# A Performer whose state is kept in a rotated basis, with weights turned on the chip

## The chip, the cores and the metric

One core of a Trainium2 chip runs the whole program; nothing is shared with other cores. The metric is device time in microseconds (us) of one execution. Everything is float32. On this core TensorE (PE) multiplies matrices, VectorE (DVE) and ScalarE (ACT) work elementwise and read its results out of PSUM, GpSimd (POOL) works on SBUF, and SyncE's queue (SP) issues nearly all DMAs.

## The reference

The input x is 8 images of 128 channels and 16 x 16 positions. Four layers follow each other; each is added to what it got, except that layer 1 adds its input inside.

```python
x = x + adder2d(group_norm(x), W)               # layer 0: -sum |W - patch|, 3x3, 128 to 128 channels
x = layer1(x)                                   # layer 1: three selective scans (f, b, s), their attention, two 3x3 convolutions
t = tokens(x)                                   # 8 x 256 tokens of 128 features
t = t + attention(ln(t)); t = t + moe(ln(t))    # layer 2
t = t + performer(ln(t))                        # layer 3, first half
t = t + spectral(ln(t))                         # layer 3, second half
```

The Performer is what most of this change touches:

```python
h = x @ tok_W + tok_b + pe
for i in range(8):
    u = layer_norm(h, ln1_g[i], ln1_b[i])       # eps 1e-5, mean and variance over the 128 features
    q, k, v = u @ Wq[i] + bq[i], u @ Wk[i] + bk[i], u @ Wv[i] + bv[i]
    ...                                         # rotary, random features (44 of each of 8 heads), linear attention
    h = h + o @ Wo[i] + bo[i]
    u = layer_norm(h, ln2_g[i], ln2_b[i])
    h = h + gelu(u @ W1[i] + b1[i]) @ W2[i] + b2[i]
    if i == 3:
        h = gelu(h @ enc_W + enc_b) @ dec_W + dec_b
return tanh(h)
```

In layer 1, for each image: `q, k, v` are the results of the three scans; `out_a = v @ softmax(q.T @ k).T` goes through a 3x3 convolution (`fuse1`, 256 to 128 channels), the gated sum of the three goes through `out_proj`, and a second 3x3 convolution (`fuse2`) takes both, 256 to 128 channels.

## The kernel before

The program runs the layers one after the other. Features lie on the 128 partitions, the 2048 tokens on the free axis, in four blocks of 512 tokens (two images each). A 128x512 result fills one bank of PSUM. A float32 product is recorded as two matmul records.

**Layer 1** (`_scans`, lines 492 to 840) walks over 192 states: 4 pairs of images, 3 branches, 16 states each. Per state DVE does two scans (L815) and a multiplication by C (L826; in the states `AWAY` POOL does it), and PE adds two products to `acc` (L834). All engines but SP follow the order of the program here (`manual_schedule`). What else has to be done is written as generators and drawn in between: `more` prepares the unit (pair and branch) after the next, and `other` runs `beside()`: norms, gates, the attention of a finished pair (`F.images`) and its two convolutions of 18 products each (`F.convolutions`). Each state has a `room` of `SHARE` = 2 products for both together, and a generator also stops for the state at every `LATER`. What is left of `other` after the last state is run in a loop behind it (L838). In `beside()` the convolutions of pairs 0 and 1 stand behind their images; those of pair 2 don't. They are drawn in `mamba_layer` (L448 to L458), after the scans, two steps for each round over the last pair's two attention generators. Behind them come the last pair's gates (`F.gated`) and convolutions. This tail is ordered by a scheduler, not by the program's order.

**The Performer** (`performer_layer`, L1002) has one generator per block, `_block`, with layer 2 in its first 30 steps. `AHEAD` takes these 30 steps of blocks 0 and 1 at the priority of layer 1's tail. Then `ORDER`, a string of 1132 digits, says which block makes its next step, and the four computing engines take their instructions in just this order. Each block has two PSUM banks of its own, and the layers' weights (`lw`) have two buffers for all blocks.

A norm (`_norm`, L1141) takes three steps: a product with `center` (identity minus 1/128) into PSUM and its squares by ACT; a product of the squares with `mean` (1/128 everywhere), Ln and Exp by ACT; and DVE's product of both, for the layers' norms followed by DVE's affine with gain and bias (L1166). For the attention's norm DVE also sums u over the tokens of an image (L1162), and `L1409` applies the affine to these sums. The block that reaches a layer first loads its weights (`_layer`, `_Layer`, L1299), 948 KB, and adds bv @ Wo to the output bias. ACT holds one function table at a time; a change between the table with Ln and Exp and the table with Gelu and Tanh is a table load (L1079).

In an attention, the step called pn below is the last product before the division: 32 records into two banks and ACT's Ln and Exp of the denominator; the steps before it transpose the query features (`turned`, L1499, records named px).

The functions that the change touches, and what calls them:

Of the kernel before, what the change touches and what calls it, by code (L numbers as in the profile page):

```python
# [45 lines left out]
RATIO = M ** -0.5  # L46
# [12 lines left out]
for _k, _n in (("q", P), ("k", P), ("v", NPAIR * (PD + 2)), ("o", P), ("w1", DFF), ("w2", DFF), ("f", HM)):  # L59
    _a = LW[next(reversed(LW))].stop if LW else 0  # L60
    LW[_k] = slice(_a, _a + _n)
# [14 lines left out]

def _constants():

    p = np.arange(P)
    c = {}  # L80
    c["ident"] = np.eye(P, dtype=np.float32)
    c["group"] = (p[:, None] // 4 == p[None, :] // 4).astype(np.float32) / 1024.0

    sel = np.zeros((P, 2, 4, NH), np.float32)
    for n in range(2):
        sel[:, n, n, :] = 0.25 * (p[:, None] // DH == np.arange(NH)[None, :])
    c["sel"] = sel.reshape(P, 8 * NH)
    c["mask"] = (np.minimum(p // M, 1)[:, None] == np.arange(PD)[None, :] // DH).astype(np.float32)
    c["pe"] = _fixed_pos_emb(P, L).T
    lpe = _fixed_pos_emb(DH, L)  # L90

    c["sin"] = np.tile(np.repeat(lpe[:, : DH // 2], 2, axis=-1).T, (NH, 1)) * np.where(p % 2, -1.0, 1.0).astype(np.float32)[:, None]
    c["cos"] = np.tile(np.repeat(lpe[:, DH // 2 :], 2, axis=-1).T, (NH, 1))
    c["more"] = np.isin(p % FG, MORE).astype(np.float32)[:, None]
    c["rev8"] = np.tile(np.arange(NE, 0, -1, dtype=np.float32), (P, 1))
    c["rev4"] = np.tile(np.arange(4, 0, -1, dtype=np.float32), (P, 1))
    return c
# [12 lines left out]
def _vectors(x):  # L110
# [19 lines left out]
    col("tok_b", x["L3_attn_tok_b"])  # L130
    col("enc_b", x["L3_attn_enc_lin_b"])
    col("dec_b", x["L3_attn_dec_lin_b"])
    for i in range(NL):
        for n in ("ln1_g", "ln1_b", "bq", "bk", "bv", "bo", "ln2_g", "ln2_b", "b1", "b2"):
            col(f"{n}{i}", x["L3_attn_" + n][i])
    return v
# [18 lines left out]
def _weights(x):  # L155
# [20 lines left out]
    for h in range(NH):  # L176
# [5 lines left out]
        [wq, wk, wv.reshape(NL, P, -1), x["L3_attn_Wo"], x["L3_attn_W1"]]  # L182
# [254 lines left out]
def mamba_layer(E):  # L437
# [3 lines left out]
    with ExitStack() as ctx:  # L441
# [7 lines left out]

        convs = F.convolutions(last - 1)  # L450
        images = [F.attention(last, b) for b in range(UB)]
        while images:
            images = [g for g in images if next(g, 0) != 0]
            for _ in range(2):
                next(convs, None)
        for p in (convs, F.gated(last), F.convolutions(last)):
            for _ in p:
                pass  # L458
# [33 lines left out]
def _scans(E, ctx, F):  # L492
# [266 lines left out]
    def beside():  # L759
# [13 lines left out]
        for p in range(NPAIRS - 1):  # L773
            yield from until((p + 1) * pair)
            if p == 1:
                yield from norm(3)
            yield from F.images(p)
            if p < NPAIRS - 2:
                yield from F.convolutions(p)
                yield from gates(p + 2)  # L780
# [221 lines left out]
def performer_layer(E, W):  # L1002
# [4 lines left out]
    with ExitStack() as ctx:  # L1007
# [18 lines left out]
        S.lw = enter("plw", 2)  # L1026
        own(2)
# [4 lines left out]
        S.lb = one.tile([P, NL], F32, tag="lb", name="lb")  # L1032
        for i in range(NL):
            nc.gpsimd.tensor_scalar_mul(S.lb[:, i : i + 1], S.v(f"ln1_b{i}"), float(L))
        S.layers = {"2": _Layer2(S)}

# [19 lines left out]
    "3213231232131213023213021023021023121301131131231231023110311131312132113211331331313331030102030213"  # L1056
    "0031203023203022020200220032030230323301332013203320323302301332303131032132302232213101231123120322"
    "3002201300220312023101311322302231312012103310233021313123020013210232112032313200331002122323212013"
    "2032302203120132202310130121023201120032013212300120011230211302132110323310133230133201233023331321"
    "0320032103232020231302023120313230131021020122102210210112101120230203201120030103112312113210132303"  # L1060
    "3131323013102012013013031233102100331003320120232021031021032013321302210220232022032120112023112031"
    "0232031200132103100133121131013121031120303130313001023213123320103203203202033220322103130103123032"
    "1302213222132211321120210212130112030230231230102011321100321103101201233010330213100231021003212203"
    "0221202032103122332322322332102210320213130112021102120130201310201133231121012001023002123112030132"
    "0212020201002102013022033222031032233203310221020302213102331223331020310330123131011203013002031230"
    "1031231112031231102312023212032123210300221030222300232312032323101203231331333032033203302121330230"
    "32330022303003321023122313133021"
# [73 lines left out]
def _norm(S, src, g=None, b=None, sums=None):  # L1141

# [4 lines left out]
    sq = S.many.tile([P, BLK], F32, tag="t", name="lsq3")  # L1147
    act(S, sq, xc, AF.Square)
# [8 lines left out]
    if sums is None:  # L1157
        nc.vector.tensor_mul(u, xc, sq)  # L1158
    else:
        for q in range(2):  # L1160
            cols = slice(q * L, (q + 1) * L)
            nc.vector.scalar_tensor_tensor(  # L1162
                u[:, cols], xc[:, cols], 1.0, sq[:, cols], ALU.mult, ALU.mult, accum_out=sums[:, q : q + 1]
            )
    if g is not None:
        nc.vector.tensor_scalar(u, u, g, b, ALU.mult, ALU.add)  # L1166
# [131 lines left out]

class _Layer:  # L1299


    def __init__(self, S, i):
        nc = S.nc
        self.w = S.lw.tile([P, LW_COLS], F32, tag="w", name=f"lw{i}")
        nc.sync.dma_start(self.w, S.dram["layers"][i])

        pb = bank(S, [P, 1], "pb3")
        S.mm(pb, self["o"], S.v(f"bv{i}"))
        self.bo = S.lw.tile([P, 1], F32, tag="bo", name="bo3")
        nc.vector.tensor_add(self.bo, pb, S.v(f"bo{i}"))  # L1310
# [5 lines left out]
def _layer(S, i):  # L1316
    if i not in S.layers:
        S.layers[i] = _Layer(S, i)
    return S.layers[i]


def _block(S):
# [10 lines left out]
        S.v("tok_b"),  # L1333
# [3 lines left out]
    )  # L1337
    yield
    for i in range(NL):
        yield from _attention(S, i, h)  # L1340
        w = _layer(S, i)
        u = yield from _norm(S, h, S.v(f"ln2_g{i}"), S.v(f"ln2_b{i}"))
# [11 lines left out]
        nc.vector.scalar_tensor_tensor(h, p2, S.v(f"b2{i}"), h, ALU.add, ALU.add)  # L1354
        yield
        if i == NL // 2 - 1:
            pz = bank(S, [LAT, BLK], "pz3")
            S.mm(pz, S.w["enc"], h)
# [5 lines left out]
            nc.vector.tensor_scalar_add(h, ph, S.v("dec_b"))  # L1364
            yield
    th = one.tile([P, BLK], F32, tag="u", name="th")
    act(S, th, h, AF.Tanh)
# [7 lines left out]
def _attention(S, i, H):  # L1375
# [8 lines left out]
    sums = one.tile([P, 2], F32, tag="us", name="us3")  # L1384
    u = yield from _norm(S, H, S.v(f"ln1_g{i}"), S.v(f"ln1_b{i}"), sums)
    w = _layer(S, i)
# [21 lines left out]

    nc.vector.tensor_scalar(sums, sums, S.v(f"ln1_g{i}"), S.lb[:, i : i + 1], ALU.mult, ALU.add)  # L1409
# [155 lines left out]
    nc.vector.scalar_tensor_tensor(H, po, w.bo, H, ALU.add, ALU.add)  # L1565
    yield

# [182 lines left out]
```

## Time and profile before

| What | Value |
|---|---|
| median of 3 runs | 3107.86 us (3105.3 to 3108.57) |
| profiled execution | 3111.2 us |
| its span | 3109.4 us |
| mean granted clock of TensorE | 0.987 |
| scans of layer 1 | 989 to 1740 us of the span |
| tail of layer 1 | 1740 to 1815 |
| layer 2 of blocks 0 and 1 alone | 1815 to 1896 |
| Performer (and the end of layer 2) | 1896 to 2866 |
| spectral layer | 2866 to 3109 |

Times inside the execution count from the start of the span. A row of a group reads: line, engine, operation, what is written and read, shapes, count | busy time in us, mean duration in ns | idle time of that engine just before, and what ended it. A matmul's duration in such a row is its latency; in a full queue the next one starts earlier, so that prices of products are taken from runs of many records. A row of a stretch reads: the stretch and its length, then the busy time and the count of PE, PE's weight loads (PEld), DVE, ACT and POOL, the granted clock, the share of the DMA engines and GB/s.

### The profile page before, as it was taken

To read this page: it belongs to the slowest core of one execution; us is meant where nothing else is said; L and a number is where in the kernel's file an instruction comes from. 1 tells how busy PE (TensorE), PEld (TensorE's weight loads), DVE (VectorE), ACT (ScalarE), POOL (GpSimd) and SP (SyncE) were. 2 spreads that over 40 slices of the span, in tenths; PEclk is the share of its full clock that TensorE was granted. 3 is DMA by queue.
4 is the path that set the end of the run, shared out by engine and by line. 5 is a ranking of instruction groups with operands and counts; after the bars stand their busy time and mean duration, and the time that the engine had idled before them with its cause. 6 is when DMAs were issued, how large, how long until landed. Compare 5 with 4: busy or idle time off the path is not lost.

```text
span 3109.4 us, 42495 instructions
## 1 busy us (share of the span) xinstructions
PE 2918.6 (94%) x16686; PEld 1294.9 (42%) x16686; DVE 2483.7 (80%) x3507; ACT 2204.1 (71%) x2634; POOL 706.1 (23%) x393
## 2 busy tenths in 40 slices
PE   6999999999999788998997889999999999999999
PEld 2333332333332233443443444455555555554444
DVE  6999999999996899999999437886877787785431
ACT  5999999999996787778777234467677777767111
POOL 3000000000000799999998200000000000000110
PEclk9999999999999899999999999999999999999999
DMA  1000000000000444344444100000000000001100
GB/s 39 1 1 5 1 1 5 1 1 5 1 1 4 167 150 144 140 152 136 138 149 136 51 28 1 13 1 14 14 13 1 14 13 1 13 1 38 54 27 14
DMA packets 39198, 131.47 MB, mean 42 GB/s; under 512 B 7491, under 2 KB 10573, under 8 KB 37589
## 3 DMA queue, kind: packets, MB, share of 16 engines
q1 hardware_dynamic: 38564, 128.02, 12.2%
q8 instruction: 131, 2.15, 0.3%
q10 hardware_dynamic: 432, 0.73, 0.1%
q14 instruction: 71, 0.57, 0.1%
HBM read 125.85 MB, written 1.84 MB: 41 GB/s over the span
## 4 chain that ended last, share of the span: by engine, by line
PE 68%; DVE 16%; ACT 7%; POOL 4%; issue 3%; DMA 1%; DVEq 0%; ACTq 0%; POOLq 0%
PE o L265 30%; PE p L265 7%; DVE st L815 5%; PE acc L265 4%; PE g L265 4%; PE conv L265 3%; PE var L265 2%; PE pf L265 2%; POOL dbu L729 2%; PE xc L265 2%; PE pc L265 2%; PE pq L265 2%; PE pn L265 1%; PE pconv L265 1%; PE px L1502 1%
## 5 line engine op out<-in xcount | busy, mean ns | idle before, releaser
L265 PE MATMUL o<-d,sel 128*32 128x512 f32 x8800 | 946.5, 592 | 5.5 <-DVE d L405 5.5
L407 ACT ACTIVATE d<-sh,w 128x2048 f32<-128x2048 f32 x460 | 886.3, 1996 | 64.3 <-PE o L265 54.4
L405 DVE TENSOR_SCALAR d<-sh,w 128x2048 f32<-128x2048 f32 x640 | 789.4, 1292 | 48.9 <-PE o L265 39.7
L729 POOL TENSOR_TENSOR dbu<-du,bs 128x1024 f32<-128x1024 f32 x191 | 447.0, 2367 | 997.3 <-DMA cs<-rows 991.4
L265 PEld LDWEIGHTS o<-d,sel 128*32 128x32 f32 x8800 | 298.2, 110 | 653.0 <-issue 541.5
L815 DVE TENSOR_TENSOR_SCAN st<-da,dbu 128x512 f32<-128x512 f32 x384 | 446.2, 1206 | 18.3 <-POOL dbu L729 15.0
L265 PE MATMUL acc<-st,cst 128*128 128x512 f32 x768 | 377.4, 623 | 62.8 <-DVE st L826 62.6
L742 ACT ACTIVATE da<-delta,neg_a 128x510 f32<-128x510 f32 x384 | 256.8, 684 | 79.0 <-DVE st L815 77.7
L265 PEld LDWEIGHTS acc<-st,cst 128*128 128x128 f32 x768 | 144.5, 196 | 264.8 <-issue 141.7
L1611 POOL COPY u<-u 128x512 f32<-128x512 f32 x4 | 2.5, 613 | 1035.3 <-DVE u L1158 1035.3
L826 DVE TENSOR_TENSOR st<-st,pcs 128x1024 f32<-128x1024 f32 x168 | 205.2, 1222 | 18.2 <-ACT pcs L734 0.8
L1079 ACT ACT_TABLE_LOAD x132 | 169.4, 1283 | 2.3
L1682 ACT COPY ug<-p 128x512 f32<-128x512 f32 x64 | 37.5, 586 | 178.2 <-PE p L265 178.2
L734 ACT COPY pcs<-cs 128x512 f32<-128x512 f32 x168 | 97.8, 582 | 54.3 <-DVE st L826 48.7
L265 PE MATMUL conv<-pad,f 128*128 128x512 f32 x288 | 132.6, 596 | 1.9 <-ACT pad L991 1.3
L265 PE MATMUL p<-g,lw 128*128 128x512 f32 x256 | 119.6, 612 | 8.8 <-ACT g L1087 8.8
L265 PE MATMUL p<-u,lw 128*128 128x512 f32 x256 | 122.6, 602 | 3.7 <-ACT g L1087 2.8
L399 DVE SCALAR_TENSOR_TENSOR d<-sh,w,d 128x2048 f32<-128x2048 f32 x52 | 122.3, 2352 | 1.9
L265 PE MATMUL p<-T,H 128*128 128x512 f32 x256 | 113.7, 596 | 4.1 <-DVE ug L1684 3.8
L265 PE MATMUL g<-ug,me 128*128 128x512 f32 (+1 forms) x320 | 112.1, 509 | 0.2 <-DVE ug L1684 0.2
L1087 ACT ACTIVATE ex<-ex 128x352 f32<-128x352 f32 x128 | 62.8, 494 | 68.5 <-DVE ex L1495 67.2
L1492 DVE TENSOR_REDUCE mq<-pq 128x8 f32<-128x352 f32 x128 | 66.4, 519 | 41.4 <-PE pq L265 41.0
(316 smaller groups left out, 4031.6 us busy)
## 6 DMA issues: line engine op xcount, KB each, us to landing
bs<-rows SPq DMA_DIRECT2D x96, 512.0 KB, 3.8
cs<-rows SPq DMA_DIRECT2D x96, 512.0 KB, 4.7
m<-in_Mphi SPq DMA_DIRECT2D x8, 1024.0 KB, 4.8
lw<-in_layers SPq DMA_DIRECT2D x8, 948.0 KB, 4.6
f<-in_fuse SPq DMA_DIRECT2D x2, 1152.0 KB, 7.5
T<-in_T SPq DMA_DIRECT2D x1, 2064.0 KB, 7.9
x<-in_x SPq DMA_DIRECT2D x4, 256.0 KB, 6.0
total<-sums SPq DMA_DIRECT2D x16, 64.0 KB, 2.0
```

The costliest lines, as they stand in the source:

```text
L265: self.nc.tensor.matmul(out, lhsT=lhsT, rhs=rhs, start=start, stop=stop)
L399: nc.vector.scalar_tensor_tensor(held, tap(k), w[:, k, f : f + 1], held, ALU.max, ALU.add)
L405: nc.vector.tensor_scalar(d, tap(k), wk, None, ALU.max)
L407: nc.scalar.activation(d, tap(k), AF.Abs, scale=-1.0, bias=wk)
L729: gen.tensor_tensor(dbs[r], got[r // NST]["du"], bc(row("bs", r), 1, 2), ALU.mult)
L734: nc.scalar.copy(pcs[r], row("cs", r))
L742: nc.scalar.activation(das[g % 3][:, :, 1:], d[:, :, 1:], AF.Exp, scale=a)
L815: nc.vector.tensor_tensor_scan(st[:, h, :], da, dbs[r][:, h, :], 0.0, ALU.mult, ALU.add)
L826: nc.vector.tensor_tensor(st, st, bc(pcs[r][:, :], 1, 2), ALU.mult)
L1079: S.tc.keep_in_program_order(S.nc.scalar.preload_act_table_set(name))
L1087: S.nc.scalar.activation(out, src, func, **kw)
L1492: nc.vector.tensor_reduce(mq, f, AX.X, ALU.max)
```

## The change

Three things are changed together.

**The basis.** The Performer's state h is kept as R.T h, where R is a Householder reflection whose last column is the constant 1/sqrt(128). The last row of the rotated state is then sqrt(128) times the mean over the features, and the other 127 rows hold the centred part. A norm therefore needs no product with `center`: the squares of the state are taken straight from SBUF, the variance is a product over 127 rows, and u is the 127 rows times the reciprocal deviation. Row 127 of u holds the constant 1, set once, and row 127 of `sums` the constant 256.

**The weights.** What reads u is turned on the chip: for Wq, Wk, Wv and for W1 a matrix `m` = R with its rows scaled by the gain, and its last column replaced by the bias, is multiplied with the weights on PE and copied back over them by ACT. Gain and bias of the norms so disappear into the weights. What writes the state (Wo, W2, tok, dec) is turned by `_outputs_turned`: a sum over the outputs and a rank-one correction on DVE and POOL. Biases and enc are turned once, in `_rotated_state`. At the end one product with R per block turns the state back for tanh. The turning of a layer's weights is three more steps in block 0's generator for each of the eight layers, and only block 0 loads them.

**The order.** `ORDER` is a new string, of 1092 digits. And the convolutions of pair 2 stand in `beside()` behind the pair's images, as those of pairs 0 and 1 do; the tail of `mamba_layer` only draws the two images, the gates and the last convolutions.

The diff, cut to its core:

```diff
@@ mamba_layer
-        convs = F.convolutions(last - 1)
         images = [F.attention(last, b) for b in range(UB)]
         while images:
             images = [g for g in images if next(g, 0) != 0]
-            for _ in range(2):
-                next(convs, None)
-        for p in (convs, F.gated(last), F.convolutions(last)):
+        for p in (F.gated(last), F.convolutions(last)):
...
@@ beside
             yield from F.images(p)
+            yield from F.convolutions(p)
             if p < NPAIRS - 2:
-                yield from F.convolutions(p)
                 yield from gates(p + 2)
...
@@ performer_layer
         S.lw = enter("plw", 2)
+        S.turn = enter("pturn", 1)
...
-        S.lb = one.tile([P, NL], F32, tag="lb", name="lb")
-        for i in range(NL):
-            nc.gpsimd.tensor_scalar_mul(S.lb[:, i : i + 1], S.v(f"ln1_b{i}"), float(L))
         S.layers = {"2": _Layer2(S)}
+        _rotated_state(S, blocks[0])
...
+def _outputs_turned(S, w, rows=P):
+    nc = S.nc
+    n = w.shape[1]
+    a, b = (S.turn.tile([P, n], F32, tag=f"t{j}{n}", name=f"turn{j}")[0:rows] for j in range(2))
+    nc.vector.tensor_reduce(a, w, AX.X, ALU.add)
+    nc.vector.tensor_scalar_mul(a, a, ROOT)
+    nc.vector.tensor_tensor(b, a, w[:, :, MEAN], ALU.subtract)
+    nc.vector.tensor_scalar_mul(b, b, ROOT / (1.0 - ROOT))
+    nc.gpsimd.tensor_tensor(w, w, bc(b, 2, P), ALU.subtract)
+    nc.gpsimd.tensor_copy(w[:, :, MEAN], a)
...
 class _Layer:
     def __init__(self, S, i):
+        self.w = S.lw.tile([P, LW_COLS], F32, tag="w", name=f"lw{i}")
+        S.nc.sync.dma_start(self.w, S.dram["layers"][i])
+
+    def turned(self, S, i):
...
+        _outputs_turned(S, self.w[:, LW["o"].start : LW["w2"].stop].rearrange("p (n d) -> p n d", d=P))
+        for n, cols in (("ln1", slice(0, LW["v"].stop)), ("ln2", LW["w1"])):
+            m = S.turn.tile([P, P], F32, tag=n, name=n + "m")
+            nc.gpsimd.tensor_scalar_mul(m, S.c("rot"), S.v(f"{n}_g{i}"))
+            nc.gpsimd.tensor_copy(m[:, MEAN:P], S.v(f"{n}_b{i}"))
+            pw = bank(S, [P, cols.stop - cols.start], "pw3")
+            S.mm(pw, m, self.w[:, cols])
+            nc.scalar.copy(self.w[:, cols], pw)
+            yield
         pb = bank(S, [P, 1], "pb3")
         S.mm(pb, self["o"], S.v(f"bv{i}"))
...
+def _state_norm(S, h, sq, u, sums=None):
+    nc = S.nc
+    rest = slice(0, MEAN)
+    var = bank(S, [P, BLK], "var3")
+    S.mm(var, S.mean[rest, :], sq[rest, :])
+    act(S, sq, var, AF.Ln, bias=S.eps)
+    act(S, sq, sq, AF.Exp, scale=-0.5)
+    yield
+    if sums is None:
+        nc.vector.tensor_mul(u[rest], h[rest], sq[rest])
+    else:
...
@@ _block
+    sq = _squares(S, h)
+    yield
+    if S.t == 0:
+        yield from _weights_of(S, 0)
+    u = one.tile([P, BLK], F32, tag="u", name="un3")
+    sums = one.tile([P, 2], F32, tag="us", name="us3")
+    nc.gpsimd.memset(u, 1.0)
+    nc.gpsimd.memset(sums, float(L))
     for i in range(NL):
-        yield from _attention(S, i, h)
-        w = _layer(S, i)
-        u = yield from _norm(S, h, S.v(f"ln2_g{i}"), S.v(f"ln2_b{i}"))
+        sq = yield from _attention(S, i, h, sq, u, sums)
+        w = S.layers[i]
+        yield from _state_norm(S, h, sq, u)
...
+        if i + 1 < NL:
+            sq = _squares(S, h)
             yield
+            if S.t == 0:
+                yield from _weights_of(S, i + 1)
+    yield
+    ph = bank(S, [P, BLK], "ph4")
+    S.mm(ph, S.c("rot"), h)
     th = one.tile([P, BLK], F32, tag="u", name="th")
-    act(S, th, h, AF.Tanh)
+    act(S, th, ph, AF.Tanh)
...
@@ _attention
-    nc.vector.tensor_scalar(sums, sums, S.v(f"ln1_g{i}"), S.lb[:, i : i + 1], ALU.mult, ALU.add)
```

The matrix R joins the constants as `rot` (128 columns), the position code is rotated on the host, in the layers' weights W1 stands before Wo so that what is turned alike lies together, and the output biases move into one group of columns, `added`.

## The prediction

> **What bounds the kernel now.** I read the page first, then the busy time by stage, then the groups of instructions with shapes kept apart, then TensorE's timeline where the last convolutions stand. Part 4 of the page, the chain of waits that ended last, says who carries the span:
>
> ```profile
> PE 68%; DVE 16%; ACT 7%; POOL 4%; issue 3%; DMA 1%; DVEq 0%; ACTq 0%; POOLq 0%
> ```
>
> The busy time of each engine by stage (PE, PE weight load, DVE, ACT, POOL, then the granted clock):
>
> ```profile
> 989.00:1740.00 751.00, 651.31 (x1533) 275.33 (x1534) 678.71 (x618) 548.62 (x907) 640.15 (x316) 0.96 0.42 141
> 1740.00:1815.00 75.00, 73.10 (x197) 35.54 (x196) 11.89 (x27) 5.79 (x19) 0.11 (x1) 1.00 0.02 3
> 1815.00:1896.00 81.00, 66.04 (x194) 31.89 (x192) 46.95 (x164) 31.55 (x64) 7.08 (x1) 0.92 0.06 24
> 1896.00:2866.00 970.00, 935.75 (x5292) 534.91 (x5291) 745.92 (x1874) 686.92 (x1097) 1.88 (x4) 1.00 0.03 9
> ```
>
> The fourth row is the Performer (with the end of layer 2): PE 96% busy, DVE 77%, ACT 71%, POOL free. There a product removed from PE is time removed, as long as DVE and ACT keep up. The second row is the tail of the state-space layer: PE alone, 73 of 75 us. The first row is the scans, where DVE has 90% and PE some room.
>
> The groups that the change touches:
>
> ```profile
> L265 PE MATMUL xc<-H,center 128*128 128x512 f32 x128 | 66.3, 601 | 0.2
> L265 PE MATMUL pn<-qp,ctx 88*32 88x256 f32 x1024 | 61.7, 381 | 0.2
> L1166 DVE TENSOR_SCALAR u<-u,vecs 128x512 f32<-128x512 f32 x64 | 35.0, 546 | 2.3
> L1409 DVE TENSOR_SCALAR us<-us,vecs,lb 128x2 f32<-128x2 f32 x32 | 9.0, 283 | 0.0
> ```
>
> An f32 product is two records, so xc is 64 products: two norms x 8 layers x 4 blocks. A record's 601 ns overlaps the next; its price in a full queue is in the chain, where 36 convolution records of this form take 15.48 us: 0.43 each, 0.86 a product.
>
> **Performer, PE.** Removed: 128 records x 0.43 = 55.0 us. Added: per layer two turned weight products (392 and 512 columns, four records, all priced as 512) 4 x 0.43 = 1.72, times 8 = 13.8; one turn back per block before tanh, 4 x 0.86 = 3.4; two small products of 18 and 10 columns once, four records at no more than the 0.27 of pg's 16 columns = 1.1. Net 18.3 - 55.0 = **-36.7 us**, nearly all on the path, since PE waits only 34 of 970 us.
>
> **Performer, DVE and ACT** (off the path while PE leads). DVE loses the affine, 35.0, and the sums' affine, 9.0. It gains per layer a reduction of 640 elements (0.69 for 512 at L922, so about 0.86) and three tiny operations of 0.17: 1.4 x 8 = 11. Net -33: from 746 to about 713. ACT copies 16 turned products, at 0.59 for 512 columns, 9; reads the state from SBUF in 64 squares, 0.63 (as lsq<-lsq) instead of 0.59, 2.6. Laid against the steps, the old order makes 132 table changes, as the trace has (1.283 us each), the new one 134: 2.6. Sum +14, to 701. Against a stage of some 930 us these are 77% and 75%: still behind PE. If that cover is gone, its price is in the third rival.
>
> **Waits for the turning.** At each of 8 turns, PE's first turned product waits for the scaled rotation, which POOL makes only after it has corrected the output weights, which wait for DVE's reduction. The chain: DVE 1.4, POOL 640 elements (1.27 for 512, 2.36 for 1024, so 1.55), small copies 0.4, the scaling 0.62 (L466), handoffs about 0.3: 4.3 us. Queued behind it on PE are the other blocks' products, and all engines wait for those. In the new order each later turn stands right after a block's pn step. That step and the transposes before it have no DVE work, so DVE is there early; pn is 32 records, 61.7 / 32 = 1.9 us, and two transposing steps are 0.6 each (75.3 us over 128) with one more product step between. That covers 3 to 4 us. I take 0.5 a turn, **+4**; bounds 0 (a wait gives nothing back) and 8 x 4.3 = 34. The 948 KB of the layer's weights (4.6 us to landing, SP's queue) need the buffer of two layers before. Between its last use and the turn stand 36 to 71 steps of about 0.86 us (970 / 1132), so the DMA is hidden; unhidden it is the slower rival.
>
> **PE's other waits**, 34 us now. Each norm loses a PE pass and an affine before its first product, and the new order leaves at least 2.7 us of other blocks' products behind the variance of every norm (Ln 0.68, Exp 0.63, product 0.69 to 0.84, handoffs). Waits that a norm ends are only a few us. I take **-2**; bounds: half of them gone, -17, or doubled, +34.
>
> The Trainium skill's SBUF — State Buffer, "SBUF: two separate sides", speaks against the change: DVE and POOL share a port pair as an exclusive lock, also against a DVE instruction with two SBUF inputs, which u = h x rstd now becomes (xc was in PSUM). A row agrees in kind:
>
> ```profile
> L1192 DVE TENSOR_SCALAR q<-q,vecs x4: 546/546/3752, 1825.3 to 1898.3; 128x512 f32<-128x512 f32 x4
> ```
>
> The 3752 fell while POOL scaled T (1821.74, 7.08 us). By the rule the turning's 2.6 us on POOL could hold DVE for at most 8 x 2.6 = 21 us; by the busy row DVE has over 200 us free, and I charge nothing.
>
> **The third convolutions.** Counting room as the scan loop does, the images of pair 2 end at state 184, so only 14 of the 36 products fit into the last seven states; the other 22 run after the last scan, and then the last pair's attention stands alone. The 14 cost nothing, as an earlier stretch shows, with two such products per state:
>
> ```profile
> 1600.88 1.88 PE L265 MATMUL conv<-pad,f 128*128 128x512 f32 x4
> 1602.60 1.88 PE L265 MATMUL acc<-st,cst 128*128 128x512 f32 x4
> 1604.31 1.88 PE L265 MATMUL conv<-pad,f 128*128 128x512 f32 x4
> 1606.03 1.88 PE L265 MATMUL acc<-st,cst 128*128 128x512 f32 x4
> ```
>
> 1.72 + 1.72 = 3.44 per state, and DVE's scans of a state come every 3.57 with or without them. The tail before, on PE:
>
> ```profile
> 1737.54 1.45 PE L265 MATMUL acc<-st,cst 128*128 128x512 f32 x3
> 1738.83 1.04 PE L908 MATMUL pt<-cst,y 128*128 128x128 f32 x8
> ...
> 1750.89 3.62 PE L265 MATMUL pa<-tok 128*128 128x256 f32 x16
> ...
> 1759.50 1.03 PE L940 MATMUL pt<-cst,at 128*128 128x128 f32 x8
> ...
> 1765.00 3.61 PE L265 MATMUL po<-att,y 128*128 128x256 f32 x16
> ...
> 1781.33 15.63 PE L265 MATMUL conv<-pad,f 128*128 128x512 f32 x36
> ```
>
> From the last acc to the fourth pair's convolutions: 1781.3 - 1738.8 = 42.5 us. After: 22 x 0.86 = 18.9; the wait between the two convolutions 1.5 (seen at 1796.4); the attention's own PE work 2.1 + 3.6 + 1.0 + 3.6 = 10.3; and its waits for copies, softmax and pads, no longer filled, about 5. Sum 35.7: **-7 us**; bounds -12 (all waits filled by gated products and layer 2) and 0 (waits twice as long). SP, DVE and ACT issue nothing new there.
>
> The clock in rows with gaps is 0.92 and 0.96. The Trainium skill (TensorE: Matmul & The Clock Gate, "What's actually happening") halves the clock after some 3.4 us idle; the attention's gaps are under 2, so by it nothing changes, and one such drop would be about 2 us.
>
> **The rest.** The rotation adds 64 KB to the constants (566.5 KB, 4.6 us to landing) ahead of the first work: +0.5. Column packing, reordered weights: nothing.
>
> **Sum.** -36.7 + 4 - 2 - 7 + 0.5 = -41.2 from the profiled execution's 3111.2: 3070.0. That execution is 3.3 above the median of 3107.86, so the forecast is **3067**.
>
> **Rivals.** *The turns lie open:* all 4.3 us of each turn stop PE, because DVE comes late to the reduction. 34 instead of 4: 3097. For it: PE takes its queue strictly in order. Against it: their place behind pn.
>
> *Slower, the turn with its load:* if the weights are loaded only when block 0 turns them, each turn adds the 4.6 of the DMA and another handoff to the 4.3, about 9.4 us with PE stopped: 75 instead of 4 gives 3138. It decides from 6.4 us a turn: (45.2 gained elsewhere + 6.2) / 8. Before, the first block to arrive loaded a layer; now only block 0 can, and the three others wait for it. Against it: the 36 to 71 steps.
>
> *DVE and ACT take over:* with less for PE, its waits double, 68 us: 3067 + 36 = 3103, no measurable change. For it: table changes and reductions stay; against it: 77% and 75%.
>
> **Chances.** Forecast 0.72 (with its own bounds, one at a time, 3042 to 3085), open turns 0.10, takeover 0.07, slower 0.09, better than 3042 0.02. The range 3042 to 3098 takes in the forecast, the open turns and little else. A measurement of this kernel tells some 0.2%, 6.2 us, from no change. Faster: 0.72 + 0.10 + 0.02 and a third of the takeover, 0.86; same 0.05; slower 0.09.
>
> **What would show it.** Right: xc<-H gone, PE's records at 0.43, the Performer stage near 930 with PE still above 94%; the tail about 68 instead of 75; the turned products' idle on PE under 8 us in sum. Wrong: PE's idle in front of the turned products over 30, or a Performer stage that keeps 960 with PE at 90%; a scan stage longer than 751.

## The result, and the profile after

The changed kernel takes 3076.78 us in the median of 4 runs (3075.53 to 3082.88), the kernel before 3108.22 on the same chip (4 runs, 3105.30 to 3111.70). The ratio is 0.9902 [0.9885, 0.9919]: 31.4 us less, where 41 were forecast. The profiled execution of after is 3075.62, its span 3073.8.

The chain of waits that ended last, in the page of after, has the shares that it had:

```profile
PE 68%; DVE 16%; ACT 7%; POOL 5%; issue 3%; DMA 1%; DVEq 0%; ACTq 0%; POOLq 0%
```

The busy time by stage of after (stretch and length, PE, PE weight load, DVE, ACT, POOL, granted clock, DMA share, GB/s):

```profile
989.00:1740.00 751.00, 653.26 (x1558) 277.02 (x1558) 678.02 (x624) 548.85 (x907) 639.82 (x312) 0.98 0.40 141
1740.00:1805.00 65.00, 59.51 (x166) 30.38 (x166) 10.81 (x23) 5.68 (x18) 0.00 (x0) 0.97 0.00 1
1805.00:1900.00 95.00, 79.52 (x230) 39.86 (x229) 54.28 (x181) 39.13 (x78) 10.74 (x10) 0.89 0.06 23
1900.00:2860.00 960.00, 919.89 (x5254) 532.59 (x5253) 731.28 (x1829) 696.01 (x1110) 31.01 (x55) 0.99 0.04 13
```

Round borders hide a few us, so the same is read between events that both traces have: the last acc product, layer 2's first xc<-X product, the first k product of the Performer, the first product of the spectral layer. The Performer between its two events, first before, then after:

```profile
1908.17:2866.53 958.36, 924.30 (x5253) 528.63 (x5252) 738.40 (x1857) 677.17 (x1081) 2.41 (x4) 1.00 0.03 9
```

```profile
1902.51:2829.84 927.33, 888.72 (x5173) 517.52 (x5173) 705.95 (x1793) 689.35 (x1098) 24.78 (x52) 0.99 0.03 10
```

PE has 80 records less and 35.6 us less work. DVE has 32 less, ACT 12 more. The stage became shorter by 31.0 only, because PE's time without work went from 958.4 - 924.3 = 34.1 to 927.3 - 888.7 = 38.6. In whole:

| Stretch | before | after | change | forecast |
|---|---|---|---|---|
| up to the last acc product | 1738.8 | 1734.8 | -4.0 | +0.5 |
| tail of layer 1, to xc<-X | 75.7 | 71.6 | -4.1 | -7 |
| layer 2 alone | 93.7 | 96.2 | +2.5 | part of the next |
| Performer | 958.4 | 927.3 | -31.0 | -34.7 |
| the rest | 242.9 | 244.0 | +1.1 | 0 |
| span | 3109.4 | 3073.8 | -35.6 | -41.2 |

The pair of traces shows 4.2 us more than the medians: the profiled execution of before lies 3.0 above its median, that of after 1.2 below. The first row is scatter as far as these traces go: besides the longer constants, two small corrections of weights and 12 products of the convolutions nothing of the change runs there, and the traces of the other runs put the same event between 1734.3 and 1741.5.

The new groups of after, with shapes kept apart, and from the page the correction of the weights:

```profile
L279 PE MATMUL pw<-lw,ln1m 128*128 128x392 f32 x16 | 7.4, 545 | 1.7 <-POOL ln1m L1343 1.7
L279 PE MATMUL pw<-lw,ln2m 128*128 128x512 f32 x16 | 8.3, 599 | 0.0
```

```profile
L1310 POOL TENSOR_TENSOR lw<-lw,turn 128x640 f32<-128x640 f32 x8 | 10.0, 1255 | 717.9 <-DVE turn L1309 626.6
```

The turned products wait 1.7 us in sum for POOL's scaled rotation; their weight loads, which come first, wait 3.9 in four turns (sum, times, longest):

```profile
PEld pw L279 <- POOL ln1m L1343: 3.9, 4, 1.5
```

And the tail of after, TensorE alone (start, length, product, count, and in brackets the idle time before it and who ended it):

```profile
1731.35 1.88 PE L279 MATMUL conv<-pad,f 128*128 128x512 f32 x4
1733.07 1.88 PE L279 MATMUL acc<-st,cst 128*128 128x512 f32 x4
1734.79 5.32 PE L279 MATMUL conv<-pad,f 128*128 128x512 f32 x12
1741.04 15.73 PE L279 MATMUL conv<-pad,f 128*128 128x512 f32 x36 [0.93 <-ACT pad L1001]
1756.61 1.91 PE L918 MATMUL pt<-cst,y 128*128 128x128 f32 x16
1759.41 3.72 PE L279 MATMUL pa<-tok 128*128 128x256 f32 x16 [0.89 <-DVE tok L883]
1765.60 1.50 PE L950 MATMUL pt<-cst,at 128*128 128x128 f32 x8 [2.47 <-DVE at L944]
1767.24 5.38 PE L279 MATMUL po<-att,y 128*128 128x256 f32 x16
1772.46 1.88 PE L279 MATMUL pm<-y,w_out_proj 128*128 128x512 f32 x4
1774.17 15.62 PE L279 MATMUL conv<-pad,f 128*128 128x512 f32 x36
```

48 convolution records, 24 products, run after the last acc, then the attention stands alone, with 2.47 us of waiting before its second transposes.

### The profile page after: what moved, and what is told of

It reads as the page before. It is cut to its first block, busy times and chain, and to the rows that moved or that the text cites. A ratio compares the mean times of both kernels' runs of the same rounds, so it can differ in the third digit from the quotient of the medians.

```text
span 3073.8 us, 42374 instructions
## 1 busy us (share of the span) xinstructions
PE 2875.2 (94%) x16602; PEld 1283.8 (42%) x16602; DVE 2451.8 (80%) x3452; ACT 2216.1 (72%) x2652; POOL 731.5 (24%) x445
## 4 chain that ended last, share of the span: by engine, by line
PE 68%; DVE 16%; ACT 7%; POOL 5%; issue 3%; DMA 1%; DVEq 0%; ACTq 0%; POOLq 0%
PE o L279 31%; PE p L279 8%; DVE st L825 5%; PE acc L279 4%; PE g L279 4%; PE conv L279 3%; POOL dbu L739 2%; PE pc L279 2%; PE var L279 2%; PE pf L279 2%; PE pq L279 2%; PE po L279 1%; PE pn L279 1%; PE pconv L279 1%; PE pa L279 1%
## 5 line engine op out<-in xcount | busy, mean ns | idle before, releaser
L279 PE MATMUL acc<-st,cst 128*128 128x512 f32 x768 | 369.4, 611 | 60.2 <-DVE st L836 59.9
L1310 POOL TENSOR_TENSOR lw<-lw,turn 128x640 f32<-128x640 f32 x8 | 10.0, 1255 | 717.9 <-DVE turn L1309 626.6
L279 PE MATMUL p<-un,lw 128*128 128x512 f32 x256 | 123.6, 605 | 3.8 <-DVE un L1381 2.1
L279 PE MATMUL pf<-lw,rk 128*128 128x352 f32 x256 | 95.4, 470 | 0.3 <-DVE ek L1525 0.2
```

Of the source, the lines that this page charges most:

```text
L279: self.nc.tensor.matmul(out, lhsT=lhsT, rhs=rhs, start=start, stop=stop)
```

## The experiments

Each ratio is to the kernel before, measured beside it. Its interval is about 0.0015 wide to either side, so two kernels are told apart from some 6 us on; below that the text says so and leans on the traces. "Over after" and "less than after" are differences of the medians. They compare different sets of runs, in which the median of before lay between 3107.1 and 3109.7. A figure for one stage comes from one trace: layer 2 with after's code took 94.0 to 96.2 us in three traces, after's Performer 926.4 to 931.9 in four.

**The convolutions' move alone,** on the kernel before:

```diff
@@ mamba_layer
-        convs = F.convolutions(last - 1)
...
-            for _ in range(2):
-                next(convs, None)
-        for p in (convs, F.gated(last), F.convolutions(last)):
+        for p in (F.gated(last), F.convolutions(last)):
@@ beside
+            yield from F.convolutions(p)
             if p < NPAIRS - 2:
-                yield from F.convolutions(p)
```

> The kernel before with the move of pair 2's convolutions alone; basis, weights and order as before. Theory (the move is worth what the two traces show from the last scan product to the first product of layer 2, 75.7 against 71.6 us): 4 us less than before, about 3104, with 12 of the 36 products inside the scans at no cost and a tail of about 71.6 us. The prediction's own figure was 7 less (3101). Rival (the move gives nothing, the difference of the two traces is chance): within 1.5 us of before, tail 75.

3104.74 us, 0.9989 [0.9979, 0.9999]: 3.2 us less, and the tail 70.9 instead of 75.7 in the trace. The interval alone would leave room for the rival's 1.5; the tail doesn't.

**The convolutions back in the tail** of after is the same edit the other way round:

> The changed kernel with pair 2's convolutions back in the tail, drawn between the last pair's attention steps; all else as changed. Theory: 4 us more than the changed kernel, about 3081, tail 75 to 76 us, the Performer unchanged at 927 us from its first k product to the first product of the spectral layer. Rival (the move also sets how layer 2 starts, through the banks and the clock): layer 2 of the first blocks, 96 us in the changed kernel and 94 before, goes back to 94 and the difference is 2 or less.

3081.69, 0.9917 [0.9902, 0.9932]: 4.9 over after, tail 74.7, Performer 927.5 as in after. From both sides the move is worth 3 to 5 us. Layer 2 did go back to 94.6, as the rival had it, but this is within what traces of the same code differ by, and the difference of the medians is not the rival's 2 or less.

**The layers' weights not turned.** The reduction, the correction, the scalings, the turned products and their copies are left out; the empty steps stay, so the order is that of after:

```diff
@@ _Layer.turned
-        _outputs_turned(S, self.w[...])
-        for n, cols in (("ln1", slice(0, LW["v"].stop)), ("ln2", LW["w1"])):
...
-            S.mm(pw, m, self.w[:, cols])
-            nc.scalar.copy(self.w[:, cols], pw)
+        for _ in range(2):
             yield
```

> The changed kernel without the turning of the layers' weights: loads, bias and the three steps of block 0 stay, DVE's and POOL's corrections, the 16 products with the scaled rotation and their copies by ACT are left out. Theory (PE binds, so its added products and its waits for them are paid in full): 16 products, 12 us at 0.43 us per 512 columns and 0.33 per 392, and some 5 us of waits, so 17 us less than the changed kernel, about 3060, and a Performer of 910 us instead of 927. Rival (the turning is hidden beside other work): within 4 us of the changed kernel.

3065.44, 0.9867 [0.9852, 0.9881]: 11.3 less than after, between the theory's 17 and the rival's 4. Layer 2 took 88.9 instead of 96.2, the Performer 923.1 instead of 927.3:

```profile
1895.91:2819.02 923.11, 882.49 (x5145) 514.36 (x5145) 696.12 (x1765) 683.06 (x1084) 4.08 (x10) 0.99 0.03 10
```

Of the eight turns the first, which stands in layer 2, costs 7.2 by these two traces, the other seven 4.2 together: 0.6 each, although each has 1.72 us of products. The clock blurs this: TensorE had half of it for 17 us of this Performer and for 10 us of after's, which hides some 3 us, so 0.6 to 1.1 each is as near as these traces come. Their cover holds. The row also shows that PE's 38.6 us without work are not the turning's: without it they are 923.1 - 882.5 = 40.6.

**The first turning early,** ahead of layer 2:

```diff
@@ performer_layer
         S.table["now"] = LN_EXP
+        for _ in _weights_of(blocks[0], 0):
+            pass
@@ _block
     if S.t == 0:
-        yield from _weights_of(S, 0)
+        for _ in range(3):
+            yield
```

> The changed kernel with the turning of layer 0's weights alone moved ahead of layer 2, outside the order string; block 0 makes three empty steps where it was. Theory (leaving the turning out brought 7 of its 11 us between the first product of layer 2 and the first k product, so it is the first turning, in a stage that is not yet full, that costs): 4 to 7 us less than the changed kernel, about 3072. Rival (all eight turnings cost the same, 1.4 us): 0 to 2 less.

3072.02, 0.9886 [0.9871, 0.9901]: 4.8 less than after. That is at the edge of what two kernels can be told apart by; the trace has layer 2 at 91.7 (96.2 in after) and the Performer at 926.4, which puts the gain where it was expected, and its tail was 1.7 shorter than after's (69.9), which the edit doesn't touch.

**The centring products again.** 64 products center x h, of the removed size, go into the variance's own bank ahead of the variance, which overwrites them:

```diff
@@ _state_norm
     var = bank(S, [P, BLK], "var3")
+    S.mm(var, S.center, h)
     S.mm(var, S.mean[rest, :], sq[rest, :])
```

> The changed kernel with one more product per norm: center times the state into the bank that the variance then overwrites, 64 products of 128x512 whose results are not used. Theory (a product on PE costs its time in this stage): 64 x 0.86 = 55 us more, 50 to 58, about 3130, all of it between the Performer's first and last product. Rival (the chain from engine to engine, or DVE and ACT, set the pace, and the gain came from the shorter chain): 0 to 20 us more, since the added product waits for nothing that the variance doesn't wait for.

3118.94, 1.0038 [1.0024, 1.0053]: 42.2 over after, for products that a full queue prices at 55.0. The row of the stage:

```profile
1905.11:2875.07 969.96, 937.49 (x5299) 542.97 (x5299) 707.47 (x1793) 693.43 (x1098) 24.79 (x52) 0.99 0.03 9
```

PE's work grew by 48.8 and its time without work shrank from 38.6 to 32.5: some of the products fell into gaps. PE's time is on the path, at 42.2 / 55.0 = 0.77 of the queue's price. The theory's 50 was too much, and the rival, that products hide in waits, is far off. The run also speaks against the new order string being simply a better one: with the centring products back it is 11.0 us slower than the kernel before, about what the turning costs.

**The affine again.** After each of the 64 norms DVE does one more pass over the normalised state:

```diff
@@ _state_norm
...
+    nc.vector.tensor_scalar(u[rest], u[rest], g[rest], b[rest], ALU.mult, ALU.add)
     yield
```

> The changed kernel with DVE's affine put back behind each of the 64 norms of the Performer, by the gain and bias that the turned weights already hold, in place on u (gains are ones and biases zeros here). Theory (DVE is not what binds, it has a fifth of the stage free): of the 35 us of DVE work less than 12 come back, 3 to 12 more than the changed kernel, since each also lengthens its norm by 0.55 us. Rival (the relief of DVE was a large part of the gain): 25 to 35 more.

3097.54, 0.9967 [0.9953, 0.9981]: 20.8 over after, for 35.0 us of DVE. It lies between the two, well above the theory's 12. The longer way from the norm to its first product could be the reason, or DVE's queue itself. So the same instructions were run with their result in a dead tile, which nothing reads (the edit against the run just told):

```diff
-    nc.vector.tensor_scalar(u[rest], u[rest], g[rest], b[rest], ALU.mult, ALU.add)
+    nc.vector.tensor_scalar(sq[rest], u[rest], g[rest], b[rest], ALU.mult, ALU.add)
```

> The changed kernel with the same 64 affines of DVE as in the run that put them back, 35 us, right behind each norm's product, but written to a tile that nobody reads, so that no product waits for them. Theory (putting them back cost 21 us because each lengthened its norm): 3 to 8 more than the changed kernel, about 3082. Rival (DVE's queue itself is close to binding, what follows on DVE comes late): 15 or more, as with the affine in place.

3096.07, 0.9955 [0.9939, 0.9970]: 19.3 over after, in the rival's range and not to be told from the version in the chain. The theory, that the longer norm made the cost, fell.

```profile
1902.99:2845.85 942.86, 895.26 (x5173) 519.84 (x5173) 738.73 (x1857) 689.63 (x1098) 25.07 (x52) 0.99 0.03 10
```

DVE is busy for 739 of 943 us, 78%, and yet 55% of what it got in addition is paid for. PE's time without work is 47.6 instead of 38.6, and its work takes 6.5 longer, of which the clock explains 5 (half of it for 20 us, 10 in after). What stands behind the affine in DVE's queue comes later, whoever it belongs to: of PE's waits over 0.15 us, those that DVE ends grew from 14.8 to 18.6 in sum, those that ACT ends from 21.7 to 26.7, although ACT got no work in addition.

**The old order** with the new code. The order is a string of block numbers, one per step. The old one was carried over: block numbers exchanged as in after, the steps of xc struck out, block 0's three turning steps put where its xc step had been.

```diff
@@ ORDER, its first line
-    "3203203322300231310203001302130303103023103020031203123012211001102001200310213200113301011301330203"
...
+    "3203230232030200031232031201231202302031003003023023012300130003030203200320033033303330131012131203"
...
```

> The changed kernel under the order string of before, carried over: blocks 0 and 1 change names, because block 1 led before and block 0 must lead now; the steps of the centring products are struck out, and block 0's three turning steps stand together where its own centring step of the attention norm stood. Theory (products less, not the new string, make the gain): 0 to 12 us more than the changed kernel, with the turnings' waits for POOL as the reason for what is lost. Rival (the new string carries a large part): 15 us or more.

3173.89, 1.0213 [1.0198, 1.0229]: 97.1 over after, where the theory had 12 at most. In the waits of the whole trace:

```profile
PE pw L279 <- POOL ln1m L1343: 34.8, 8, 5.6
```

34.8 us in eight turns is 4.35 a turn, the 4.3 of the rival with open turns. The turned products themselves, in the view of their tile (least, median and longest duration in ns):

```profile
L279 PE MATMUL pw<-lw,ln1m x16: 492/861/1022, 1897.4 to 2756.4; 128*128 128x392 f32 x16
L279 PE MATMUL pw<-lw,ln2m x16: 697/1061/1160, 1898.6 to 2757.9; 128*128 128x512 f32 x16
```

Their medians are 861 and 1061 where after has 545 and 592. Beside each of the eight turns the granted clock was one half for a while; it was so for 58 us of this Performer in sum (10 in after), some 38 of them at the seven turns that stand in it. So a wait of 4.35 us costs more than 4.35. The Trainium skill, TensorE: Matmul & The Clock Gate, "What's actually happening", lets the clock fall to half after an idle window of about 3.4 us. Seven of the eight waits, 3.8 to 5.6 us, agree with this; the eighth was 2.5 us, and the clock was one half behind it too.

**The old order without the turning** joins the two edits, to see what remains of the difference when no turn can wait:

> The order of before, carried over as in the run with the old order, and the turning of the layers' weights left out (corrections, products with the scaled rotation, copies). To be set beside the run without turning under the new order, 3065. Theory (what the old order lost, 97 us, were the open turnings: 35 us of PE's waits for POOL, some 24 us of the half clock that follows them, and what queued up behind): without them the two orders are within 12 us, 3065 to 3077. Rival (the new string fits the new steps and the old one doesn't): 25 us or more above 3065.

3107.68, 0.9994 [0.9984, 1.0003]. Against the same code in the new order (3065.44) that is 42.2 more, the rival's side, and against the kernel before it is nothing.

```profile
1904.81:2863.35 958.54, 884.84 (x5134) 507.08 (x5132) 697.07 (x1761) 678.75 (x1081) 4.11 (x10) 0.99 0.03 11
```

The stage is as long as in the kernel before (958.4), with 39.5 us less work on PE, 41 less on DVE and 1.6 more on ACT. All of it became waiting: 958.5 - 884.8 = 73.7 us without work instead of 34.1. The largest of PE's waits in this stretch:

```profile
PE p L279 <- ACT g L1095: 16.3, 16, 2.4
PE pl L279 <- ACT sqq L1095: 7.6, 9, 1.7
PE pf L279 <- DVE ek L1518: 4.7, 8, 0.9
PE pg L279 <- DVE dm L1535: 4.6, 6, 2.3
```

They are many and short, after four different steps; in the kernel before the first two kinds are 11.6 and 6.6. Of the waits over 0.15 us, those that DVE ends grew from 11.0 to 35.8 in sum, those that ACT ends from 21.4 to 35.7. My theory, that both orders would do alike, fell.

**The old order with the scaling first.** POOL makes both scaled rotations before it corrects the output weights, so that the turned products need not wait for DVE's reduction:

```diff
@@ _Layer.turned
+        ms = []
+        for n in ("ln1", "ln2"):
...
+            ms.append(m)
         _outputs_turned(S, self.w[...])
-        for n, cols in (("ln1", slice(0, LW["v"].stop)), ("ln2", LW["w1"])):
...
+        for m, cols in zip(ms, (slice(0, LW["v"].stop), LW["w1"])):
```

> The old order with the turning, but POOL scales the two rotations before it corrects the output weights, so that PE's first turned product waits for 0.8 us of POOL that depend on nothing, and no longer for DVE's reduction and 3 us of POOL. Theory: of the old order's 3174 the 33 us of waits and most of the 24 us of half clock go, 3105 to 3120, the waits of the turned product for POOL below 5 us. Rival (the turnings stop PE for other reasons, the copies by ACT or the step of block 0): above 3140.

3146.16, 1.0116 [1.0101, 1.0131]: 27.7 less than in the old order as it was, but above the rival's 3140 and not the theory's 3105 to 3120. The wait of the turned products is gone; a part of it moved to the third turning step, the bias through the corrected Wo (in the Performer):

```profile
PE pb L279 <- POOL lw L1311: 14.0, 6, 3.3
```

The chain from DVE's reduction over POOL is the cause of the turned products' wait, then, and to reorder POOL's part takes away less than half of the 66.2 us that the turning costs under the old order (3173.9 - 3107.7, the run above); the turning in after costs 11.3. Of the 38.5 us that are left over the run without turning, the Performer has 35.5 (994.05 against 958.54): 12.8 of PE's waiting and 22.7 of its work, the turned products (7 x 1.72 = 12.0) and more time at the half clock (38 us against 14).

**The second late convolution in the tail's gaps.** Pair 2's first convolution stays in the scans, its second is drawn between the steps of the last attention:

```diff
@@ mamba_layer
+        convs = F.convolutions(last - 1, (1,))
...
+            next(convs, None)
-        for p in (F.gated(last), F.convolutions(last)):
+        for p in (convs, F.gated(last), F.convolutions(last)):
@@ beside
-            yield from F.convolutions(p)
+            yield from F.convolutions(p, (0, 1) if p < NPAIRS - 2 else (0,))
...
```

> The changed kernel, but of pair 2's convolutions only the first stands in the chain beside the scans; the second is drawn in the tail, three of its products between every two steps of the last pair's attention. Theory (in the tail PE waits some 7 us while the attention stands alone): the tail falls from 71.6 to about 65 us, 6 to 7 us less than the changed kernel, about 3070. Rival (the tail is bound by the attention's chain, whatever stands between): within 2 us.

3074.85, 0.9896 [0.9881, 0.9911]: 1.9 less than after, which can't be told from nothing, nor from the 6 expected. In the trace the tail did shrink, from 71.6 to 64.4, with the attention's steps back to back:

```profile
1748.55 3.62 PE L279 MATMUL pa<-tok 128*128 128x256 f32 x16
1752.00 2.74 PE L279 MATMUL conv<-pad,f 128*128 128x512 f32 x6
1754.58 1.09 PE L952 MATMUL pt<-cst,at 128*128 128x128 f32 x8
1755.50 2.74 PE L279 MATMUL conv<-pad,f 128*128 128x512 f32 x6
1758.08 3.62 PE L279 MATMUL po<-att,y 128*128 128x256 f32 x16
```

**All three additions to after** (second convolution in the gaps, scaling first, first turning early), in the new order:

> The changed kernel with three edits together: pair 2's second convolution drawn in the tail between the attention's steps, the rotations scaled before the corrections, the first layer's weights turned ahead of layer 2. The first alone had a tail 7 us shorter, the third alone a stretch up to the spectral layer 5 us shorter. Theory (they add): 9 to 14 less than the changed kernel, 3063 to 3068. Rival (what the tail gives is lost again when layer 2 starts): 3 to 6 less, as the third alone, about 3072.

3065.99, 0.9858 [0.9844, 0.9873]: 10.8 less than after, as expected, and the fastest kernel of this study with nothing left out. Tail 64.4, layer 2 87.7, Performer 926.6.

## Why the prediction was right, and where it was 10 us too good

The direction, the place and the order of size were right, and 3076.8 lies in the range. By its own steps:

**Performer, PE: -36.7, the work nearly right.** PE's work fell by 35.6 in the Performer and rose by 2.1 in layer 2, where the first turn and the small products stand: 33.5 in sum. "Nearly all on the path" was too much by a quarter: put back into after, the products cost 0.77 of their queue price.

**PE's other waits: -2, the step that failed.** The norms lost a product and an affine each, and the waits did not become less but more: 34.1 us before, 38.6 in after, 40.6 with the turning left out, when nothing of it can be the turning's. (Four traces of after's Performer have 38.4 to 38.8, two of before's 33.9 and 34.1, so this is not scatter.) So this term is about +6.5, within its own bounds (-17 to +34) but of the other sign.

**The sum came nearer than its terms.** Outside the turning, layer 2 and the Performer gained 40.0 us (before against the run without turning) where 50.5 + 2 = 52.5 were summed: 9.4 of the gap is waits, 3.1 PE's work. The turning cost 11.4 there by the same traces where 13.8 + 4 = 17.8 was summed. So an error of 12.5 was half hidden by one of 6.4 the other way, and that is luck. Nor do the forecast's bounds, 3042 to 3085, follow from its terms "one at a time": the largest single steps down and up, -17 and +34 for PE's other waits, give 3052 and 3103.

**DVE and ACT off the path, 0: wrong as a rule.** I argued from 77% and 75% busy. The two affine runs show that 55 to 59% of 35 us put on DVE is paid at 78% busy. The 32 us that the change takes from DVE are therefore not worthless; what they were worth in this change can't be read off, since the removed work of both engines, 50.5 us of PE's queue (55.0 less the turns back and the small products) and 44 of DVE, brought only 40.0 us together (1052.0 for layer 2 and Performer before, 1012.0 without the turning). The prices of added work hold for work added to an order that was not made for it; they don't add up to the gain of removing it.

**The orders were taken as alike; they are not.** I weighed the new order only for table changes and for cover behind pn. With the carried-over order none of the removed work is gained (3107.7 against 3109.7 before, although this version has the convolutions' gain and no turning), with the new one 42 us are, the convolutions' 3 to 5 among them. The runs show that the order decides between these two; they don't show that no other carrying-over of the old one would do better.

**Waits for the turning: +4, too dear in the stage, too cheap at its start.** The seven turns behind pn cost 0.6 to 1.1 each, waits and products together, where 1.72 of products and 0.5 of wait were priced. The first, in a stage where PE has room but is also waited for, costs 5 to 7. All eight cost 11.3 by the medians.

**Third convolutions: -7, mis-sized; -3 to -5.** 24 products were left after the last acc, not 22, because the last state's two stand behind its acc. They took 21.8 us with the wait between the two convolutions, where 18.9 + 1.5 = 20.4 was summed (that wait is 0.93 in after and 0.99 before, not 1.5). The attention alone took 15.9 instead of 15.3, of which 1.8 is the clock: po's 16 records took 5.38 us, 3.62 before. And the sum left out the product of out_proj (pm), 1.7 us. From the last acc to the fourth pair's convolutions it is 39.4 against 42.5 before, not 35.7. The gap before the attention's second transposes was 2.47, not under 2, and "by it nothing changes" failed, for one drop of the size that was named.

**The port lock, 0: right as a price, untested as a rule.** The rule, Trainium skill, SBUF — State Buffer, "SBUF: two separate sides", would show as single long u = h x rstd instructions. No run here shows one: all 32 of the second norms' took 672 to 694 ns in after. But none of them ran while POOL was at work. Where affines of layer 2's norms on DVE fell beside POOL at the first turn, two took 0.99 and 0.91 us instead of 0.55, as under such a lock. The first of them:

```profile
1892.78 1.26 POOL L1310 TENSOR_TENSOR lw<-lw,turn 128x640 f32<-128x640 f32 x1 [71.17 <-DVE turn L1309]
1893.33 0.99 DVE L1189 TENSOR_SCALAR q<-q,vecs 128x512 f32<-128x512 f32 x1
```

**The rivals.** The open turns have the right wait, 4.35 a turn, but only under the old order, and there the turning costs 66.2 us in all, not the 13.8 + 34 of products and waits. The turn with its load: no run shows PE waiting for the weights' DMA. The takeover: PE's time without work grew by 4.5 us instead of doubling, though the price of the affine shows that this rival was nearer than its two percentages said.

**What stays open.** What in the new order makes the 6.5 us of PE's added waits is not shown. They are DVE's: of PE's waits over 0.15 us, those that ACT ends are 21.4 before and 21.7 without the turning, those that DVE ends 11.0 and 17.7. The largest of the new ones is the attention's output product behind the division (po, 4.6 without the turning, 0.3 before), the rest is spread. Nor is it shown whether the second late convolution alone gains its 7 us: its tail does, but the Performer of that one trace, the same code as in after, was 4.6 longer (931.9), with TensorE at the half clock for 20 us of it instead of 10. The other pair of traces of one Performer code differs by 3.5 (1055.5 and 1052.0 for layer 2 with Performer, with the convolutions moved and before).

## What to carry to other kernels

Where four chains share in-order engines by an order written out by hand, work that is removed may be gained only with an order made for the new steps: here one order gained 42 us, the other nothing. Cost the order as a part of the change. An engine's busy share does not say what its work costs: put the disputed instructions back, once in the chain and once aside, and read the price. A chain of some 4 us over two slower engines cost 0.6 to 1.1 us a turn behind other products, its own products included, and 8.3 (66.2 / 8) where it stood open.

## What was not expected of the hardware

The clock fell to half in after's tail without any single wait as long as the 3.4 us of the page cited above: between 1763.1 and 1767.2 PE had 1.5 us of transposes and two waits, the longer 2.47, and po's records then took 5.38 us instead of 3.62. The granted clock of the two stretches that hold them is 0.76:

```profile
1766.00:1769.00 3.00, 2.80 (x12) 2.01 (x11) 1.79 (x4) 0.00 (x0) 0.00 (x0) 0.76 0.00 0
1769.00:1773.00 4.00, 4.00 (x15) 3.11 (x14) 0.00 (x0) 0.99 (x4) 0.00 (x0) 0.76 0.00 0
```

Such a stretch does not always do it: in the traces of three other runs (the convolutions' move alone, the first turn early, no turning) the same transposes stand behind the same wait of 2.47, and po took 3.69. What decides is not shown. With the gaps filled by products (the second late convolution) po took 3.62. And an operation that no one waits for cost about as much as the same one in the chain, 19.3 and 20.8 us for 64 times 546 ns.
